# Statistics of layer 1 on the scalar engine, and a second transpose by blocks and transfers, in a one-core Newton and convolution kernel

## The chip, the core and the metric

The kernel runs on one core of a Trainium2 chip. The core has five engines with a queue each, and each queue is worked off in order: TensorE (PE, matrix products, written to PSUM), VectorE (DVE), ScalarE (ACT), GpSimd (POOL) and SyncE (SP, which here only issues DMA transfers). Sixteen DMA engines carry the transfers. The metric is the time of the device for one execution, in microseconds. The profile shows one such execution; its span is the part of it that the profiler records.

## The reference

The input x is 32 images of 32 channels of 128x128, in float32. Two layers are applied, each on a group norm with 16 groups of two channels.

```
# layer 0: x = x + sqrtm(gn(x)), five Newton-Schulz steps for each channel's 128x128 matrix
normA = sqrt(sum(A * A)); Y = A / normA; Z = I
for _ in range(5):
    T = 0.5 * (3 I - Z @ Y)
    Y = Y @ T; Z = T @ Z
sA = Y * sqrt(normA)

# layer 1: x = x + spectral_conv(gn(x)): a 2-D transform (real part), 64 x 32 modes kept,
# a product over channels with one 32x32 matrix for each mode, and the transform back
```

The group norm of layer 1 needs, for each group, the mean and the variance of what layer 0 gave.

## The kernel before

**Units.** One unit of work is four channels of one image, a tile of 128x512 (P, 4, P). There are 256 units, 8 for each image. `newton` (lines 446 to 478) runs the whole iteration of one unit as a Python generator: each `yield` ends its turn, and `yield from rest` gives up two turns. The iteration is not done step by step as in the reference: two polynomial stages, each through a quartic (`near_quartic` or `far_quartic`), and a last product give the same result.

**Rounds and lanes.** The main loop (from line 1077) goes round eight lanes. In each round every lane with a unit advances by one turn, and between lanes the other generators advance: `preps` (statistics of layer 0 for a pair of images), `norms` (normalising the inputs), `posts` (`settle` for a finished unit, then `forward`, `summed`), `specs`, `prods` and `backs` (layer 1). A new unit starts every 23/8 rounds where `is_far` holds, which is for images 1 to 18 (144 units), and every 5 rounds else (112 units). The order in which this loop emits instructions is the order on every engine (`keep_in_program_order`); no engine can overtake. What an engine has to give within a round's time decides whether PE, which is the fullest, finds its operands ready: two rounds lie between the product and the product that reads its result after one `rest`, four after two.

**A far unit, turn by turn.** `far_quartic` (421 to 442): four products of `mb` and `m` into a PSUM bank; DVE adds them to `v`; DVE transposes v by blocks of 32x32 into a tile `turn` (the `nc.vector.transpose` of line 426); four DMA transfers issued by SP (429 to 435) put the blocks into `w`, which then is, in another order of columns, the transpose of v; POOL takes mb from a multiple of the identity; after two rests PE multiplies v and w, and DVE makes `q`. In `newton`, ACT writes y (line 453) and the new m (456) from PSUM; after a rest PE transposes m with the identity (line 458: `transposed(m)`, four PE instructions) and ACT copies that out of PSUM as the new `mb`; POOL makes the new v (460); a rest; then `far_quartic` again, then the last products, and DVE adds the result to `xt` (line 475).

**After a unit.** `settle` (483 to 499) stores xt to DRAM (`mid`, from SP), lets POOL fold it for the transform, and lets DVE take two `bn_stats` of 128x256, one for each group, into `b_st`. After the eighth unit of an image `summed` (536 to 567) turns these into the group norm's scale: `moments` (199 to 215) takes means with a small product on PE, then DVE works out squares, and small products on PE sum over partitions. `forward` transforms four units at a time and `spectrum` goes on from there.

**Buffers.** PSUM is eight banks of 128x512, taken in turn by `bank()`. Tiles of a unit come from `four(tag, more)` with the number of buffers in `rooms` (309, 310): mb has 2 + 3, turn 4, xt 10 + 4 in the first part of the kernel. Tile reuse makes waits by itself. Each DMA transfer counts up one of eight semaphores, taken in turn by SP's and ACT's transfers together, and waits for the transfer eight before it. ACT issues the loads of the inputs (`fetch`, line 367, two for each unit, and `load` in `prep`, one for each unit on average).

Of the kernel before, what the change touches and what calls it, by code (L numbers as in the profile page):

```python
# [36 lines left out]
P = 128  # L37
# [17 lines left out]
EYE_V = 3.375 * SV  # L55
EYE_Q = 24.609375 * SQ
QS = 16 * SQ
FIRST = GROUPS[0] - 1
MORE = FIRST * 8 + 6
NB = 8  # L60
# [34 lines left out]
def conv_preact_kernel(  # L95
# [19 lines left out]
    nc.vector.tensor_scalar_mul(eye1[:, 0, :], ident, EYE)  # L115
    eye = eye1.to_broadcast([P, 4, P])
    eyes = []
    for n, f in (("v", EYE_V), ("q", EYE_Q)):
        e = const.tile([P, 1, P], F32, name=f"eye_{n}")
        nc.vector.tensor_scalar_mul(e[:, 0, :], ident, f)  # L120
        eyes.append(e.to_broadcast([P, 4, P]))
    eye_v, eye_q = eyes
    avg_mean = const.tile([P, P], F32, name="avg_mean")
    nc.vector.memset(avg_mean, -1.0 / 512)

    avg_v = const.tile([P, 1], F32, name="avg_v")
    nc.vector.memset(avg_v, 0.5 / (P * P))
    avg_0 = const.tile([P, 1], F32, name="avg_0")
    nc.vector.memset(avg_0, -P * P / 256)


    mid = [dram.tile([P, C, P], F32, name=f"mid{b}", tag=f"mid{b}") for b in range(B)]
# [66 lines left out]
    def moments(st, ms, tag):  # L199

        n = st.shape[1]
        f = st.rearrange("p g (e t) -> p g e t", t=3)
        nc.vector.tensor_reduce(ms, f[:, :, :, 1], AX.X, ALU.add)
        yield from pause
        pm = bank()[:, 0, 0:n]
        nc.tensor.matmul(pm, avg_mean, ms, start=True, stop=True)
        nm = small.tile([P, n], F32, tag=f"{tag}_nm", name=f"{tag}_nm", bufs=2)
        nc.vector.tensor_scalar_mul(nm, pm, 2.0)
        d = small.tile([P, n, 2], F32, tag=f"{tag}_d", name=f"{tag}_d")
        nc.vector.tensor_tensor(  # L210
            d, f[:, :, :, 1], nm[:, :, None].to_broadcast([P, n, 2]), ALU.add
        )
        nc.vector.tensor_mul(d, d, d)
        nc.vector.scalar_tensor_tensor(d, d, 128.0, f[:, :, :, 2], ALU.mult, ALU.add)
        return nm, d
# [4 lines left out]
    def kept(issued):  # L220
        return issued

    def prep(bs, made):
# [75 lines left out]
        for far in sorted({is_far(b) for b in bs}):  # L299
            of = [k for k, b in enumerate(bs) if is_far(b) == far]  # L300
            c = slice(of[0] * C, of[-1] * C + C)
            f = EYE_Q * QS if far else EYE * QF
            nc.vector.tensor_scalar_mul(nn[:, c], nn[:, c], P * (1.5 / f) ** 2)
        yield
        yield from root(nn, nc_, sn)
# [24 lines left out]
    def plus(ps, f, t, tag, more):  # L330

        s = four(tag, more)
        nc.vector.scalar_tensor_tensor(s, ps, f, t, ALU.mult, ALU.add)
        return s
# [17 lines left out]
    def transposed(t):  # L352
        ps = bank()
        for j in range(4):
            nc.tensor.transpose(ps[:, j, :], t[:, j, :], ident)
        return ps
# [61 lines left out]
        yield from rest  # L418
        return q

    def far_quartic(m, mb, v, more):

        ps = products(mb, m)
        nc.vector.scalar_tensor_tensor(v, ps, 1 / (4.5 * MS), v, ALU.mult, ALU.add)
        t = four("turn", more)
        nc.vector.transpose(blocks(t), v.rearrange("p c (i b) -> p b c i", b=4))
        w = four("w", more)
        into = w.rearrange("p c x -> p (c x)").rearrange("p (a x) -> p a x", a=4)
        for a in range(4):
            src = t[32 * a : 32 * a + 32].rearrange("p c x -> p (c x)")  # L430
            kept(
                nc.sync.dma_start(
                    out=into[:, a], in_=src.rearrange("p (b x) -> p b x", b=4)
                )
            )
        minus(eye_q, mb, mb)
        yield from rest
        yield from rest
        ps = products(v, blocks(w).rearrange("p a c j -> p c a j"))
        q = plus(ps, SQ / SV**2, mb, "q", more)  # L440
        yield from rest
        return q

# [2 lines left out]
    def newton(g, sn, xt, m, mb, v, far, more):  # L446


        qf, et, eye_t = (QS, EYE_Q, eye_q) if far else (QF, EYE, eye)
        q = yield from far_quartic(m, mb, v, more) if far else near_quartic(m, mb, more)  # L450
        my = four("my", more)
        y = my[:, :, 0, :]
        nc.scalar.mul(y, products(q, m), 1 / (MS * qf))
        yield from rest
        m = my[:, :, 1, :]
        nc.scalar.mul(m, products(q, y), MS / qf)
        yield from rest
        mb = taken(transposed(m), "mb", more)
        if far:
            v = minus(eye_v, m, four("v", more))  # L460
        yield from rest
        q = yield from far_quartic(m, mb, v, more) if far else near_quartic(m, mb, more)
        both = [bank().rearrange("p (j k) x -> p j k x", k=2) for _ in range(2)]
        for j in range(4):
            nc.tensor.matmul(both[j // 2][:, j % 2], q[:, j], my[:, j], start=True, stop=True)
        w, y = four("t", more), four("y4", more)
        for h in range(2):
            nc.scalar.mul(w[:, 2 * h : 2 * h + 2, :], both[h][:, :, 1, :], 1 / (MS * qf))
        for j in range(4):
            c = 4 * g + j  # L470
            nc.scalar.mul(y[:, j, :], both[j // 2][:, j % 2, 0, :], sn[:, c : c + 1])
        yield from rest
        t = plus(products(w, q), -0.5 * et / (1.5 * qf), eye_t, "t", more)
        yield from rest
        nc.vector.tensor_tensor(xt, products(t, y), xt, ALU.add)
        if not todo and lanes.count(None) == LANES - 1:
            warm(2)
        yield
# [4 lines left out]
    def settle(b, g, st, xt):  # L483

        kept(nc.sync.dma_start(out=mid[b][:, 4 * g : 4 * g + 4, :], in_=xt))
        if g % 2 == 0:
            folds[b, g // 2] = sets.tile([P, 8, P], F32, tag="fold", name=f"fold{b}_{g}", bufs=3)
        f = folds[b, g // 2][:, 4 * (g % 2) : 4 * (g % 2) + 4, :]
        for half, op in enumerate((ALU.add, ALU.subtract)):
            nc.gpsimd.tensor_tensor(  # L490
                f[:, :, 64 * half : 64 * half + 64], xt[:, :, 0:64], xt[:, :, 64:128], op
            )
        for j in range(2):
            at = 8 * (g // 2 % 2) + 4 * (g // 4) + 2 * (g % 2) + j
            nc.vector.bn_stats(
                st[:, at, :], xt[:, 2 * j : 2 * j + 2, :].rearrange("p c h -> p (c h)")
            )
        settled.append(rounds)
        yield
# [35 lines left out]

    def summed(b, st):

        mq = small.tile([P, 2, G], F32, tag="b_mq", name=f"b_mq{b}")
        _, d = yield from moments(st, mq[:, 0, :], "b")
        yield  # L540

        nc.vector.tensor_reduce(mq[:, 1, :], d, AX.X, ALU.add)
        wide = small.tile([P, 2, G, 2], F32, tag="b_wide", name=f"b_wide{b}")
        nc.vector.tensor_copy(wide, mq[:, :, :, None].to_broadcast([P, 2, G, 2]))
        wide = wide.rearrange("p k g c -> p k (g c)")
        yield from pause
        pv = bank()[:, 0, :]
        for i in range(4):
            rows = slice(C * i, C * i + C)
            nc.tensor.matmul(pv[rows, 0:1], wide[:, 1, :], avg_v, start=True, stop=True)  # L550
        nc.tensor.matmul(pv[0:C, 1:2], wide[:, 0, :], avg_0, start=True, stop=True)
        v = small.tile([P, 2], F32, tag="b_v", name=f"b_v{b}")
        nc.vector.tensor_scalar(v[:, 0:1], pv[:, 0:1], 1.0, EPS, ALU.mult, ALU.add)
        nc.vector.tensor_copy(v[0:C, 1:2], pv[0:C, 1:2])
        yield
        s = small.tile([P, 3], F32, tag="b_r", name=f"b_r{b}")
        nc.scalar.activation(s[:, 0:1], v[:, 0:1], AF.Sqrt)
        yield
        nc.vector.reciprocal(s[:, 1:2], s[:, 0:1])
        nc.vector.tensor_scalar(  # L560
            s[:, 2:3], v[:, 0:1], s[:, 1:2], s[:, 1:2], ALU.mult, ALU.mult
        )
        nc.vector.tensor_scalar(s[:, 2:3], s[:, 2:3], -0.5, 1.5, ALU.mult, ALU.add)
        r = small.tile([P, 1], F32, tag="b_inv", name=f"b_inv{b}")
        nc.vector.tensor_mul(r, s[:, 1:2], s[:, 2:3])
        scales[b] = v, r
        yield
# [460 lines left out]
    def end(b, g, xt):  # L1028

        if g == 0:  # L1030
            u = up.tile([P, 2, 8, 2, L], F32, tag="u", name=f"u{b}")
            st = small.tile([P, G, 6], F32, tag="b_st", name=f"b_st{b}", bufs=2)
            ended[b] = (u, st)
        u, st = ended[b]
        posts.append(settle(b, g, st, xt))
        if g == C // 4 - 1:
            posts.append(then(summed(b, st)))
        if g % 4 == 3:
            posts.append(forward(b, g // 4, u))
        if g == C // 4 - 1:  # L1040
            posts.append(last(b, u))
# [144 lines left out]
```

## Time and profile before

| | |
|---|---|
| median of 3 runs | 3018.94 us (3016.51 to 3023.95) |
| the profiled execution | 3016.65 us, of which the span is 3014.7 us |
| PE busy | 2897.6 us, 96% of the span |
| PE weight loads busy | 2689.0 us |
| DVE busy | 2321.8 us, 77% |
| POOL busy | 1995.8 us, 66% |
| ACT busy | 1652.1 us, 55% |
| DMA packets | 442482, 560.91 MB |
| chain that ended last | PE 71%, POOL 8%, DVE 7%, DMA 7%, issue 5% |

The span has two parts. Up to some 1650 us the far units run, and each stretch of 100 us has the same look: PE busy for 99 to 100 of it, DVE for 83 to 91, POOL for 71 to 75, ACT for 58 to 62, and the DMA engines for 49 to 65%. After that come the near units together with layer 1's products and inverse transforms: PE is busy for 90 to 100 of 100 us, DVE for 50 to 84, ACT for 44 to 61, and the DMA engines for up to 85%. Busy time of an engine is the union of its instructions; a busy PE is not a PE at its peak, but where one product follows the other without a gap nothing more fits in between. All lines of the kernel are put down to line 89, where a helper issues every instruction, so groups are told apart by the names of their tiles: "turn<-v" is an instruction that reads v and writes turn.

### The profile page before, as it was taken

What the parts mean: (1) busy time and instruction counts of PE and PEld (TensorE: products, weight loads), DVE (VectorE), ACT (ScalarE), POOL (GpSimd) and SP (SyncE); (2) the same over time, 40 slices, a digit from 0 to 9 for tenths busy, and PEclk for the clock granted to TensorE, in tenths of its full rate; (3) what the DMA queues carried; (4) which work ended last, traced back from release to release, by engine and by line L of the source; (5) the groups of instructions that cost most, each with busy time, mean ns of one, the idle gap of its engine ahead of it and who ended that gap; (6) DMA issues with size and microseconds to landing.
All of it is one profiled execution on the core that took longest, in us unless ns stands there. A gap on an engine that the chain in (4) does not pass through costs nothing.

```text
span 3014.7 us, 73315 instructions
## 1 busy us (share of the span) xinstructions
PE 2897.6 (96%) x27112; PEld 2689.0 (89%) x27112; DVE 2321.8 (77%) x4262; ACT 1652.1 (55%) x4187; POOL 1995.8 (66%) x2308
## 2 busy tenths in 40 slices
PE   7999999999999999999999999999989999999995
PEld 7899999999999999999999889888878899888884
DVE  7778898989888888889876645777886767776564
ACT  4566666566565656566554445455544544665452
POOL 4676777777777767777765434787777763678352
PEclk9999999999999999999999999999999999999997
DMA  5465655556565656565633566777877737676576
GB/s 176 135 176 145 171 163 153 167 152 180 134 192 135 192 131 195 142 183 140 190 102 99 158 209 208 257 247 254 271 235 245 252 121 225 203 242 216 175 230 242
DMA packets 442482, 560.91 MB, mean 186 GB/s; under 512 B 99344, under 2 KB 260112, under 8 KB 442128
## 3 DMA queue, kind: packets, MB, share of 16 engines
q1 hardware_dynamic: 328512, 347.77, 38.7%
q10 hardware_dynamic: 113616, 208.45, 22.2%
q8 instruction: 218, 3.57, 0.5%
q14 instruction: 136, 1.11, 0.1%
HBM read 326.93 MB, written 153.62 MB: 159 GB/s over the span
## 4 chain that ended last, share of the span: by engine, by line
PE 71%; POOL 8%; DVE 7%; DMA 7%; issue 5%; SPq 1%; ACT 1%; ACTq 0%; POOLq 0%; DVEq 0%
PE ps L89 71%; POOL yt L89 3%; POOL r L89 2%; POOL x L89 1%; POOL fold L89 1%; DMA yt<-mid 1%; SPq L89 1%; DVE turn L89 1%; DVE root L89 1%; DMA w<-turn 1%; DMA out<-yt 1%; DVE v L89 1%; DVE yt L89 1%; DVE a_d L89 1%; DMA xs<-in_xs 1%
## 5 line engine op out<-in xcount | busy, mean ns | idle before, releaser
L89 PE MATMUL ps<-my,q 128*128 128x128 f32 (+1 forms) x4096 | 747.0, 330 | 16.6 <-DVE q L89 9.9
L89 PEld LDWEIGHTS ps<-my,q 128*128 128x128 f32 x4096 | 623.0, 192 | 67.7 <-issue 7.4
L89 PE MATMUL ps<-w,v 128*128 128x128 f32 x4096 | 555.4, 279 | 19.6 <-DVE w L89 15.3
L89 ACT ACTIVATE b<-b,a_off,a_sc 128x128 f32<-128x128 f32 x1024 | 469.7, 491 | 166.2 <-issue 57.0
L89 ACT ACTIVATE my<-ps 128x512 f32<-128x512 f32 x512 | 306.2, 599 | 428.3 <-PE ps L89 408.9
L89 POOL TENSOR_TENSOR fold<-xt 128x256 f32<-128x256 f32 x512 | 363.4, 731 | 261.5 <-DVE xt L89 248.9
L89 PEld LDWEIGHTS ps<-w,v 128*128 128x128 f32 x4096 | 502.9, 193 | 32.5 <-DVE w L89 13.9
L89 POOL TENSOR_TENSOR yt<-yt,d 128x512 f32<-128x512 f32 x244 | 306.5, 1279 | 223.2 <-ACT d L89 195.5
L89 ACT ACTIVATE t<-ps 128x256 f32<-128x256 f32 x512 | 192.0, 381 | 311.7 <-PE ps L89 298.4
L89 DVE STREAM_TRANSPOSE turn<-v 128x512 f32<-128x512 f32 x288 | 326.1, 1132 | 9.9
L89 POOL TENSOR_SCALAR x<-xt,a_nm,a_sc 128x128 f32<-128x128 f32 x736 | 321.4, 450 | 15.6 <-DVE a_sc L89 15.4
L89 POOL TENSOR_TENSOR mb<-eye_q,mb 128x512 f32<-128x512 f32 x144 | 184.0, 1278 | 197.8 <-ACT y L89 139.2
L89 ACT ACTIVATE y<-ps,a_t_s 128x128 f32<-128x128 f32 x1024 | 290.4, 374 | 0.0
L89 POOL TENSOR_TENSOR v<-eye_v,x 128x512 f32<-128x512 f32 x144 | 184.0, 1278 | 143.8 <-ACT x L89 136.7
L89 PE MATMUL ps<-q,t 128*128 128x128 f32 x2048 | 273.9, 277 | 4.3 <-ACT t L89 3.7
L89 PE MATMUL ps<-x,b 128*128 128x128 f32 x2048 | 277.7, 279 | 0.0
L89 PE MATMUL ps<-x,q 128*128 128x128 f32 x2048 | 274.7, 277 | 3.0 <-DVE w L89 2.0
L89 DVE SCALAR_TENSOR_TENSOR v<-ps,v 128x512 f32<-128x512 f32 x288 | 195.1, 678 | 104.5 <-PE ps L89 101.8
L89 PE MATMUL ps<-y,t 128*128 128x128 f32 x2048 | 274.5, 277 | 0.1
L89 PE MATMUL ps<-my,mb 128*128 128x128 f32 x2048 | 272.2, 276 | 0.0
L89 PEld LDWEIGHTS ps<-my,mb 128*128 128x128 f32 x2048 | 257.9, 192 | 9.6 <-issue 1.6
L89 PEld LDWEIGHTS ps<-x,q 128*128 128x128 f32 x2048 | 249.4, 192 | 14.1 <-issue 8.4
(131 smaller groups left out, 5074.9 us busy)
## 6 DMA issues: line engine op xcount, KB each, us to landing
w<-turn SPq DMA_DIRECT2D x1152, 64.0 KB
b<-in_x ACTq DMA_DIRECT2D x256, 256.0 KB
xt<-in_xt ACTq DMA_DIRECT2D x256, 256.0 KB
mid<-xt SPq DMA_DIRECT2D x256, 256.0 KB
yt<-mid SPq DMA_DIRECT2D x128, 512.0 KB
xs<-in_xs ACTq DMA_DIRECT2D x252, 256.0 KB
out<-yt SPq DMA_DIRECT2D x115, 512.0 KB
plain<-in_wk SPq DMA_DIRECT2D x34, 512.0 KB
```

What stands on the lines that cost most here:

```text
L89: return self.tc.keep_in_program_order(issue(*args, **kw))
```

## The change

Two things are changed, and the first stage's iteration gets other scales for it.

- Statistics of layer 1. `settle` no longer has `bn_stats`. For each of the unit's two groups ACT runs two activations over 128x256 of xt: a Copy, whose accumulator output is the sum, and a Square with the group's (negative) mean of layer 0 as bias, whose accumulator output is the sum of squares about that mean. The elements themselves go into a tile `waste` that nothing reads. The second group's pair comes a turn later. `summed` no longer calls `moments`; it has sums of both kinds at once, copies them and the mean into `wide` (three copies on DVE), sums over partitions on PE (13 small products for each image, 5 and one of 128x16 before), and gets the variance on DVE.
- The second mb of a far unit. PE's four transposes of m and ACT's copy are gone. DVE transposes the products of q and y by blocks straight out of PSUM into a turn tile, right after ACT has been given m from the same bank, and four DMA transfers from SP put the blocks into mb, now in runs of 32 elements. The rests around it are kept. Since PSUM holds the products and not m, mb comes with another scale (`TURNED`), which the second quartic takes into account; a third identity, `eye_p`, belongs to it. Near units keep PE's transposes.

Beside this `a_nm`, the means of layer 0, has three buffers in place of two.

```diff
-    nc.vector.memset(avg_0, -P * P / 256)
+    nc.vector.memset(avg_0, -0.5)
+    avg_s = const.tile([P, 1], F32, name="avg_s")
+    nc.vector.memset(avg_s, 1 / P)
+    waste = const.tile([P, 2 * P], F32, name="waste")
...
-    def far_quartic(m, mb, v, more):
+    def across(t, into):
+        for a in range(4):
+            src = t[32 * a : 32 * a + 32].rearrange("p c x -> p (c x)")
+            kept(
+                nc.sync.dma_start(out=into(a), in_=src.rearrange("p (b x) -> p b x", b=4))
+            )
+
+    def far_quartic(m, mb, v, more, f, eye_q):
...
         w = four("w", more)
...
+        across(t, lambda a: w.rearrange("p c x -> p (c x)")[:, P * a : P * a + P])
...
         m = my[:, :, 1, :]
-        nc.scalar.mul(m, products(q, y), MS / qf)
-        yield from rest
-        mb = taken(transposed(m), "mb", more)
+        ps = products(q, y)
+        nc.scalar.mul(m, ps, MS / qf)
         if far:
+            t = four("turn", more)
+            nc.vector.transpose(blocks(t), ps.rearrange("p c (i b) -> p b c i", b=4))
+            mb = four("mb", more)
+            across(t, lambda a: mb[:, :, 32 * a : 32 * a + 32])
+            yield from rest
             v = minus(eye_v, m, four("v", more))
-        yield from rest
-        q = yield from far_quartic(m, mb, v, more) if far else near_quartic(m, mb, more)
+            yield from rest
+            qf, et, eye_t = QS * TURNED, EYE_Q * TURNED, eye_p
+            q = yield from far_quartic(m, mb, v, more, TURNED, eye_p)
+        else:
+            yield from rest
+            mb = taken(transposed(m), "mb", more)
+            yield from rest
+            et, eye_t = EYE, eye
+            q = yield from near_quartic(m, mb, more)
...
         for j in range(2):
-            at = 8 * (g // 2 % 2) + 4 * (g // 4) + 2 * (g % 2) + j
-            nc.vector.bn_stats(
-                st[:, at, :], xt[:, 2 * j : 2 * j + 2, :].rearrange("p c h -> p (c h)")
-            )
+            if j:
+                yield
+            of = xt[:, 2 * j : 2 * j + 2, :].rearrange("p c h -> p (c h)")
+            n = 2 * g + j
+            nc.scalar.activation(
+                waste, of, AF.Copy, accum_out=st[:, 0, at + j : at + j + 1]
+            )
+            nc.scalar.activation(
+                waste,
+                of,
+                AF.Square,
+                bias=made[b][0][:, n : n + 1],
+                accum_out=st[:, 1, at + j : at + j + 1],
+            )
...
-        mq = small.tile([P, 2, G], F32, tag="b_mq", name=f"b_mq{b}")
-        _, d = yield from moments(st, mq[:, 0, :], "b")
-        yield
-
-        nc.vector.tensor_reduce(mq[:, 1, :], d, AX.X, ALU.add)
-        wide = small.tile([P, 2, G, 2], F32, tag="b_wide", name=f"b_wide{b}")
-        nc.vector.tensor_copy(wide, mq[:, :, :, None].to_broadcast([P, 2, G, 2]))
+        wide = small.tile([P, 3, G, 2], F32, tag="b_wide", name=f"b_wide{b}")
+        nc.vector.tensor_copy(wide[:, 0:2], st[:, :, :, None].to_broadcast([P, 2, G, 2]))
+        for half in range(2):
+            nm = made[b][0].rearrange("p (a h c) -> p h a c", a=2, h=2)[:, half]
+            nc.vector.tensor_copy(
+                wide[:, 2, 8 * half : 8 * half + 8].rearrange("p (a c) e -> p a c e", a=2),
+                nm[:, :, :, None].to_broadcast([P, 2, 4, 2]),
+            )
...
             nc.tensor.matmul(pv[rows, 0:1], wide[:, 1, :], avg_v, start=True, stop=True)
+            nc.tensor.matmul(pv[rows, 2:3], wide[:, 0, :], avg_v, start=True, stop=False)
+            nc.tensor.matmul(pv[rows, 2:3], wide[:, 2, :], avg_s, start=False, stop=True)
```

More of the change, by code (lines that the diff above doesn't have):

```diff
@@ L57 @@
 QS = 16 * SQ
+TURNED = QS / MS
 FIRST = GROUPS[0] - 1
@@ L117, in conv_preact_kernel @@
     eyes = []
-    for n, f in (("v", EYE_V), ("q", EYE_Q)):
+    for n, f in (("v", EYE_V), ("q", EYE_Q), ("p", EYE_Q * TURNED)):
         e = const.tile([P, 1, P], F32, name=f"eye_{n}")
@@ L121, in conv_preact_kernel @@
         eyes.append(e.to_broadcast([P, 4, P]))
-    eye_v, eye_q = eyes
+    eye_v, eye_q, eye_p = eyes
     avg_mean = const.tile([P, P], F32, name="avg_mean")
@@ L206, in moments @@
         nc.tensor.matmul(pm, avg_mean, ms, start=True, stop=True)
-        nm = small.tile([P, n], F32, tag=f"{tag}_nm", name=f"{tag}_nm", bufs=2)
+        nm = small.tile([P, n], F32, tag=f"{tag}_nm", name=f"{tag}_nm", bufs=3)
         nc.vector.tensor_scalar_mul(nm, pm, 2.0)
@@ L301, in prep @@
             c = slice(of[0] * C, of[-1] * C + C)
-            f = EYE_Q * QS if far else EYE * QF
+            f = EYE_Q * QS * TURNED**2 if far else EYE * QF
             nc.vector.tensor_scalar_mul(nn[:, c], nn[:, c], P * (1.5 / f) ** 2)
@@ L419, in near_quartic @@
         return q
-    def far_quartic(m, mb, v, more):
+    def across(t, into):
[5 more added lines that the diff above has]
+    def far_quartic(m, mb, v, more, f, eye_q):
         ps = products(mb, m)
-        nc.vector.scalar_tensor_tensor(v, ps, 1 / (4.5 * MS), v, ALU.mult, ALU.add)
+        nc.vector.scalar_tensor_tensor(v, ps, 1 / (4.5 * MS * f), v, ALU.mult, ALU.add)
         t = four("turn", more)
@@ L427, in far_quartic @@
         w = four("w", more)
[L428 to L433, printed above, removed]
-                )
-            )
+        across(t, lambda a: w.rearrange("p c x -> p (c x)")[:, P * a : P * a + P])
         minus(eye_q, mb, mb)
@@ L439, in far_quartic @@
         ps = products(v, blocks(w).rearrange("p a c j -> p c a j"))
-        q = plus(ps, SQ / SV**2, mb, "q", more)
+        q = plus(ps, f * SQ / SV**2, mb, "q", more)
         yield from rest
@@ L446, in newton @@
     def newton(g, sn, xt, m, mb, v, far, more):
-        qf, et, eye_t = (QS, EYE_Q, eye_q) if far else (QF, EYE, eye)
-        q = yield from far_quartic(m, mb, v, more) if far else near_quartic(m, mb, more)
+        qf = QS if far else QF
+        if far:
+            q = yield from far_quartic(m, mb, v, more, 1.0, eye_q)
+        else:
+            q = yield from near_quartic(m, mb, more)
         my = four("my", more)
@@ L455, in newton @@
         m = my[:, :, 1, :]
-        nc.scalar.mul(m, products(q, y), MS / qf)
-        yield from rest
-        mb = taken(transposed(m), "mb", more)
+        ps = products(q, y)
+        nc.scalar.mul(m, ps, MS / qf)
         if far:
-            v = minus(eye_v, m, four("v", more))
-        yield from rest
-        q = yield from far_quartic(m, mb, v, more) if far else near_quartic(m, mb, more)
+            t = four("turn", more)
[3 more added lines that the diff above has]
+            yield from rest
+            v = minus(eye_v, m, four("v", more))
+            yield from rest
+            qf, et, eye_t = QS * TURNED, EYE_Q * TURNED, eye_p
+            q = yield from far_quartic(m, mb, v, more, TURNED, eye_p)
+        else:
+            yield from rest
+            mb = taken(transposed(m), "mb", more)
+            yield from rest
+            et, eye_t = EYE, eye
+            q = yield from near_quartic(m, mb, more)
         both = [bank().rearrange("p (j k) x -> p j k x", k=2) for _ in range(2)]
@@ L492, in settle @@
             )
+        at = 8 * (g // 2 % 2) + 4 * (g // 4) + 2 * (g % 2)
         for j in range(2):
-            at = 8 * (g // 2 % 2) + 4 * (g // 4) + 2 * (g % 2) + j
-            nc.vector.bn_stats(
-                st[:, at, :], xt[:, 2 * j : 2 * j + 2, :].rearrange("p c h -> p (c h)")
+            if j:
[11 more added lines that the diff above has]
+                accum_out=st[:, 1, at + j : at + j + 1],
             )
@@ L550, in summed @@
             nc.tensor.matmul(pv[rows, 0:1], wide[:, 1, :], avg_v, start=True, stop=True)
+            nc.tensor.matmul(pv[rows, 2:3], wide[:, 0, :], avg_v, start=True, stop=False)
+            nc.tensor.matmul(pv[rows, 2:3], wide[:, 2, :], avg_s, start=False, stop=True)
         nc.tensor.matmul(pv[0:C, 1:2], wide[:, 0, :], avg_0, start=True, stop=True)
-        v = small.tile([P, 2], F32, tag="b_v", name=f"b_v{b}")
-        nc.vector.tensor_scalar(v[:, 0:1], pv[:, 0:1], 1.0, EPS, ALU.mult, ALU.add)
+        v = small.tile([P, 4], F32, tag="b_v", name=f"b_v{b}")
+        nc.vector.tensor_copy(v[:, 2:3], pv[:, 2:3])
         nc.vector.tensor_copy(v[0:C, 1:2], pv[0:C, 1:2])
+        nc.vector.tensor_scalar(v[:, 3:4], v[:, 2:3], v[:, 2:3], -1.0, ALU.mult, ALU.mult)
+        nc.vector.tensor_scalar(v[:, 0:1], pv[:, 0:1], EPS, v[:, 3:4], ALU.add, ALU.add)
         yield
@@ L1031, in end @@
             u = up.tile([P, 2, 8, 2, L], F32, tag="u", name=f"u{b}")
-            st = small.tile([P, G, 6], F32, tag="b_st", name=f"b_st{b}", bufs=2)
+            st = small.tile([P, 2, G], F32, tag="b_st", name=f"b_st{b}", bufs=2)
             ended[b] = (u, st)
```

## The prediction

> **What bounds the kernel now.** I read the page first, then busy time by windows, the timeline of PE, what PE waited for, and the groups of instructions by shape.
>
> ```profile
> span 3014.7 us, 73315 instructions
> PE 2897.6 (96%) x27112; PEld 2689.0 (89%) x27112; DVE 2321.8 (77%) x4262; ACT 1652.1 (55%) x4187; POOL 1995.8 (66%) x2308
> ...
> 300.00:1500.00 1200.00, 1194.07 (x9977) 1133.43 (x9976) 1037.99 (x1837) 730.05 (x1870) 873.30 (x960) 1.00 0.59 163
> ```
>
> The last row is a stretch of the far units: length, then busy PE, PEld, DVE, ACT, POOL, clock, DMA share, GB/s. PE has 6 us of 1200 free, DVE 13%, ACT 39%. The chain that ended last has a period there:
>
> ```profile
> 1090.08 118.98 PE ps L89 x970
> ...
> 1250.25 118.98 PE ps L89 x972
> ```
>
> 160.2 us for two images (16 units), so 10.01 us for a unit. What PE's four transposes cost is read from starts, since matmuls overlap:
>
> ```profile
> 1004.32 1.06 PE L89 MATMUL ps<-w,v 128*128 128x128 f32 x8
> 1005.21 0.60 PE L89 MATMUL ps<-ident,my 128*128 128x128 f32 x4
> 1005.64 1.06 PE L89 MATMUL ps<-my,q 128*128 128x128 f32 x8
> ```
>
> From 1005.21 to 1005.64: 0.43 to 0.44 us, under half of four products. What PE waited for in 300 to 1500, then DVE in the worst stretch of a period:
>
> ```profile
> PE ps L89 <- DVE a_d L89: 2.9, 7, 0.4
> PE ps L89 <- DVE q L89: 2.3, 7, 0.3
> PE ps L89 <- ACT my L89: 0.8, 1, 0.8
> ...
> 1200.00:1256.00 56.00, 55.28 (x468) 52.45 (x467) 53.36 (x93) 35.48 (x93) 39.64 (x45) 1.00 0.49 131
> ```
>
> PE hardly waits, but DVE is the one it waits for: the seven waits on a_d and on q come once a period, where `prep`'s small operations pile onto DVE. In these 56 us DVE waits 1.5 us in all. From the end of DVE's q to the next product that reads it there are often 3 us, but in this stretch 0.1 to 2; behind ACT's m, t and mb there are usually 4 to 5 (starts and ends of the trace). So PE sets the pace, DVE is a hair behind, ACT has room. The rows for the change:
>
> ```profile
> L89 DVE STREAM_TRANSPOSE turn<-v 128x512 f32<-128x512 f32 x288 | 326.1, 1132 | 9.9
> L89 DVE BATCH_NORM_STATS2 b_st<-xt 128x6 f32<-128x256 f32 x512 | 189.6, 413 | 0.3
> L89 ACT COPY mb<-ps 128x512 f32<-128x512 f32 x256 | 149.7, 585 | 177.8 <-PE ps L89 161.7 <-DMA w<-turn 6.1 <-POOL yt L89 2.5
> L89 DVE STREAM_TRANSPOSE u<-ps 128x512 f32<-128x512 f32 x64 | 45.5, 710 | 12.9 <-PE ps L89 12.8
> ...
> L89 SPq DMA_DIRECT2D w<-turn x1152: 542/602/1984, 90.8 to 1556.4; - x192
> ```
>
> [...] ACT's d and DVE's yt read one bank, and ACT waited 20.8 us, 37 times, for DVE yt. So DVE's new transpose waits for ACT's m. [...] The trace has 381 for t<-ps with 256 elements[...]. [...] The packet records here show 34.7 ns for 512 bytes, 18.5 for 256 and 13.1 for 128.
>
> **The change, part by part.** Sums are against the profiled execution (3016.65 us with 3014.7 in the span; the median is 2.3 us higher).
>
> PE: 144 far units lose 0.436 us, −62.8 us; a far period becomes 160.2 − 16 x 0.436 = 153.2 us. The eight more tiny products of an image follow each other at some 10 ns an instruction, so +0.2 us an image: 5 us in all at most, mostly in PE's gaps; I take nothing.
>
> DVE, for a period: 138.8 us busy. Away: 32 `bn_stats` (11.9 us at 0.37 busy), and for each image moments and squares (some 1.9 us, less 1.1 for the copies and the variance that come): −13.5. New: 16 block transposes from PSUM. No row has a strided read of PSUM. Low end 0.71 us (u<-ps, no stride penalty)[...]; I take 1.2[...]: +19.2[...]. DVE then has 144.5 us of 153.2, 94%. The average fits, the bad stretch doesn't: PE would now need 56 − 56/10.01 x 0.436 = 53.6 us for it, DVE's 53.4 lose 10 `bn_stats` and an image's moments (−4.5) and gain 5.6 transposes and the new copies (+7.5): 56.4, and 0.1 us was left ahead of PE. The 2.8 us of excess come out as waiting of PE, and up to 1.5 more if DVE's own waits stay (2.8 to 4.3). I take 3.5 x 9 periods = +31.5 us (at 0.71 for a transpose: 0.7 us, +6[...]).
>
> ACT, for a unit: 6.1 us; mb away in far units, −0.585. New: two Copies[...] and two Squares with a bias pointer[...], each waiting for the one before it because of `waste`[...], plus whatever the accumulator's read-out costs. No row shows that; I take 0.1 to 0.25 us for each of four (bounds 0 and 0.5): 2.2 to 2.8. ACT goes to 7.7 to 8.3 of 9.57 us, plus some 0.3 where it issues DMAs: 84 to 90%. It stays under PE, but its queue now blocks in two new places: the first Copy waits for DVE's xt (at that place in ACT's order ACT came before xt was ready in 30 of 120 far units, by up to 2.7 us), and y, m and t stand behind. Their slack of 4 to 5 us hides most. I take +5 us in far units. In the near part nothing leaves PE; 112 units put 0.25 of ACT's time more in, where t has 3.2 us to spare at the median, 1.6 at its worst twentieth, and DVE loses 0.74 us a unit. I take +10 us (from −10, where DVE's w and t held PE, to +30).
>
> SP and DMA: twelve rather than eight transfers for a unit; at 0.62 us an issue SP goes from some 5.5 to 7.9 us of 9.57. Their 512-byte runs become 128 bytes: 2048 packets x 13.1 ns / 16 = 1.7 us of all engines a unit (2.4 at the 256-byte price), so the share goes from 0.59 to about 0.80. mb has four rounds (13.3 us); DVE's lag of 2 to 5, its transpose, four issues (2.5) and the landing (2.3, up to 6.8) make 8 to 13: hidden, barely at its worst. As a transfer waits for the eighth before it, ACT's loads stand behind w's sooner: 5 to 6 us of PE's time after it rather than 8 to 9. I count that in ACT's 5 us. `turn` has four buffers for three uses a unit (two before), 12.8 us of reuse against some 7 of life.
>
> Sum: −62.8 + 31.5 + 5 + 10 = −16.3, 3000.4 us; at the level of the median 3002.
>
> **Rivals.** *The full gain.* [...] DVE then has less work than before and PE keeps 153.2 us: −63 + 6 + 5 = −52, 2967. For it: u<-ps at 710. Against: turn<-v at 1132. *A wash.* DVE waits for ACT's m whenever it is up to date, and its 9 free microseconds a period go to that (16 x 0.5): the period stays near 160, 3010 to 3028. *Slower: ACT paces.* The four statistics with their read-outs, and the waits of an in-order queue for xt and for earlier transfers, reach 4.2 us a unit; 5.5 + 0.3 + 4.2 = 10.0 is today's pace, so from there on far units are slower than before, and the near part pays in full. At 4.6 us: +0.4 x 144, +20 near, −10 for what waits coincide: 3085; about 3050 at 4.3. For it: ACT waits on DVE and DVE on ACT in turn. [...] *Transfers late.* The DMA share stands at 0.92 in the worst 10 us of a period; with 0.2 more it is full for some 60 us of each, mb and the loads land late: 4 us past the gain in each period, 3035.
>
> **How the numbers follow.** DVE takes half (2985 to 3010): 0.36. Full gain (2950 to 2985): 0.10. Wash: 0.14. ACT paces (3028 to 3080): 0.30. Transfers late (3028 to 3050): 0.10. Runs of this kernel spread by 0.25%, so 0.3% (9 us) tells from no change: faster 0.46, same 0.14, slower 0.40. The range leaves out half of the full gain and the upper part of ACT's case: 2965 to 3055. The likeliest case's own range is 2985 to 3010.
>
> **What would show it.** Right: far periods of 156 to 158 us; DVE over 92% there, turn<-ps near 1.2 us; new waits of PE on DVE q and a_d of 3 to 4 us a period, nothing on mb's transfers; ACT at 80 to 85%. Wrong: waits of PE on ACT my or t; DVE's turn waiting for ACT my by more than 10 us a period; a second period above 160; mb<-turn issues well above 0.62 us on SP.

## The result and the profile after

The changed kernel takes 3107.8 us (3103.5 to 3111.1), against 3018.4 (3016.5 to 3024.0) for the kernel before: a ratio of 1.029, 95% interval 1.027 to 1.031. It is 89 us slower. 3002 was forecast.

In the two profiled executions all of it lies in the far units. The last transfer into w is issued at 1644.2 us instead of 1556.4, 87.8 us later; what follows it takes 1457.5 us instead of 1458.3. The page of the changed kernel, its stretch from 300 to 1500 us (length, then busy PE, PEld, DVE, ACT, POOL, granted clock, DMA share, GB/s), and what PE waited for there (total, times, longest):

```profile
span 3101.7 us, 75862 instructions
PE 2877.4 (93%) x26984; PEld 2649.5 (85%) x26984; DVE 2214.0 (71%) x3832; ACT 2050.5 (66%) x6091; POOL 1996.9 (64%) x2308
...
PE 54%; DMA 14%; POOL 9%; DVE 6%; issue 6%; ACT 6%; SPq 4%; ACTq 1%; DVEq 0%; POOLq 0%
...
300.00:1500.00 1200.00, 1106.56 (x9118) 1039.77 (x9118) 955.77 (x1587) 836.12 (x2551) 820.52 (x903) 0.98 0.72 177
```

```profile
PE ps L90 <- ACT my L90: 43.5, 12, 6.2
PE ps L90 <- DMA mb<-turn: 13.9, 9, 2.9
PE ps L90 <- DVE q L90: 13.6, 10, 2.0
PE ps L90 <- DVE xt L90: 6.8, 8, 1.0
PE ps L90 <- DMA w<-turn: 5.9, 8, 1.3
```

No engine is full in this stretch: PE 92%, DVE 80%, ACT 70%, POOL 68%, the DMA engines 72%. PE had 6 us free before and has 93 now. In the chain that ended last PE fell from 71% to 54% and DMA rose from 7% to 14%. So nothing replaced PE as the bound. What PE waits for comes late, most of all ACT's m. The rows of what the change added, grouped by shape, with busy time and mean ns of one, then the idle time before it; of SP the issues, shortest, median and longest:

```profile
L90 DVE STREAM_TRANSPOSE turn<-ps 128x512 f32<-128x512 f32 x144 | 102.4, 711 | 165.6 <-ACT my L90 145.3 <-DMA w<-turn 20.0
L90 ACT ACTIVATE waste<-xt 128x256 f32<-128x256 f32 x512 | 216.7, 423 | 83.8 <-DVE v L90 18.1 <-DMA mb<-turn 9.9 <-DMA b<-in_x 9.3
L90 ACT ACTIVATE waste<-xt,a_nm 128x256 f32<-128x256 f32 x512 | 260.4, 509 | 16.6
L90 ACT ACTIVATION_READ_ACCUMULATOR waste<-xt 128x1 f32 x512 | 104.1, 203 | 0.0
L90 ACT ACTIVATION_READ_ACCUMULATOR waste<-xt,a_nm 128x1 f32 x512 | 95.5, 186 | 0.0
...
L90 SPq DMA_DIRECT2D w<-turn x1152: 542/602/2265, 94.0 to 1644.2; - x192
L90 SPq DMA_DIRECT2D mb<-turn x576: 609/632/3177, 114.2 to 1632.4; - x192
```

The own prices of the additions are small: 0.711 us for the block transpose out of PSUM, and for a pair of statistics 0.423 + 0.203 + 0.509 + 0.186, of which neighbours overlap somewhat.

**One stall, followed back.** One of PE's long waits for ACT's m shows how it comes about. The timelines of PE, ACT and SP in the changed kernel (start, length, engine, what, and in brackets the idle time before it with its releaser):

```profile
1045.91 1.09 PE L90 MATMUL ps<-fold,tab 128*32 128x504 f32 x12
1051.52 2.08 PE L90 MATMUL ps<-my,q 128*128 128x128 f32 x8 [4.52 <-ACT my L90]
...
1041.92 5.96 ACTq L90 DMA_DIRECT2D xs<-in_xs  x3
1047.92 0.49 ACT L90 ACTIVATE b<-b,a_off,a_sc 128x128 f32<-128x128 f32 x1 [5.84 <-DMA mid<-xt]
...
1049.09 0.40 ACT L90 ACTIVATE waste<-xt 128x256 f32<-128x256 f32 x1
...
1050.89 0.57 ACT L90 ACTIVATE my<-ps 128x512 f32<-128x512 f32 x1
...
1040.19 4.80 SPq L90 DMA_DIRECT2D mb<-turn  x4
1045.04 0.63 SPq L90 DMA_DIRECT2D mid<-xt  x1
```

PE waits 4.5 us for ACT's m. ACT stood 5.8 us at a load of xs, issued at 1047.54. By the instruction records the 3469 transfers of SP and ACT count on eight semaphores, and this load on the same one as SP's store of xt into mid before it, of which the chain has the landing at 1047.52. SP issued that store only at 1045.04, behind four transfers of mb that held SP for 4.8 us (the chain has their first released by POOL's x, at 1041.98). After that ACT works off what had piled up: three normalisations, a pair of statistics, two more, and then m, 3 us after it was free. SP's lateness has passed into ACT through a semaphore, with no data between them.

This is no single case. Between 300 and 1500 us PE waits seven times for ACT's m for 4.5 to 6.2 us, once in every period of 16 units; these make 36.6 of its 43.5 us. Each of the seven ends 3.6 us after a stop of ACT, of 5.5 to 7.1 us, for the landing of a store into mid (total, times, longest):

```profile
ACT b L90 <- DMA mid<-xt: 47.5, 10, 7.1
```

The stall then costs more than itself. The same stretch in windows of 2 us, with PE first (busy, matmuls) and the granted clock third from the end:

```profile
1046.00:1048.00 2.00, 1.00 (x12) 0.31 (x12) 2.00 (x5) 0.08 (x1) 0.00 (x0) 1.00 0.82 228
1048.00:1050.00 2.00, 0.00 (x0) 0.00 (x0) 1.17 (x4) 1.97 (x6) 0.00 (x0) 1.00 0.86 248
1050.00:1052.00 2.00, 0.48 (x2) 0.48 (x3) 0.94 (x2) 1.47 (x5) 1.25 (x2) 0.71 0.73 194
1052.00:1054.00 2.00, 2.00 (x11) 2.00 (x11) 0.00 (x0) 0.37 (x1) 1.25 (x2) 0.50 0.46 143
1054.00:1056.00 2.00, 2.00 (x12) 2.00 (x11) 1.74 (x4) 1.27 (x5) 0.61 (x1) 0.50 0.45 140
1056.00:1058.00 2.00, 2.00 (x12) 2.00 (x12) 1.31 (x2) 0.68 (x2) 2.00 (x3) 0.58 0.55 76
1058.00:1060.00 2.00, 2.00 (x13) 1.79 (x12) 1.65 (x2) 0.80 (x2) 1.63 (x3) 1.00 0.95 245
```

From 1050.8 to 1057.6 us PE has half its clock: 11 or 12 matmuls in 2 us, where the windows of 2 us from 1060 to 1066 us, at full clock, have 21 each. From its first matmul at 1051.5 on that is some 3 us lost on top of 4.5. Between 300 and 1500 us the clock is at half nine times, four times for 3.41 us and five times for 6.83, which makes 47.8 us. Seven of the nine follow the waits for ACT's m, but two follow waits of only 2.2 and 2.9 us. All nine begin on one grid of 3.41 us. In the step of the grid just before, PE was busy for nothing at the seven, and for 58 and 27% at the two, so the clock fell there without a whole step of idle time. The kernel before has none in that stretch.

The sum for that stretch: 93.4 us idle against 5.9, and 0.02 of 1200 = 24 us of clock (some 3 of them while PE stood anyway), so at most 112 lost more; 0.436 us for each of some 114 units saved, 50 (9118 PE instructions at 80.2 a unit; before 9977 for 119.9 units, so 83.2, less four and plus one). Net at most 62 in 1200 us, or 0.54 for a unit and 78 for 144, against 85 measured from the first to the last transfer into w.

### The profile page after: what moved, and what is told of

Read it like the earlier page. It is cut to its first block, busy times and chain, and to the rows that moved or that the text cites. A ratio compares the mean times of both kernels' runs of the same rounds, so it can differ in the third digit from the quotient of the medians.

```text
span 3101.7 us, 75862 instructions
## 1 busy us (share of the span) xinstructions
PE 2877.4 (93%) x26984; PEld 2649.5 (85%) x26984; DVE 2214.0 (71%) x3832; ACT 2050.5 (66%) x6091; POOL 1996.9 (64%) x2308
## 4 chain that ended last, share of the span: by engine, by line
PE 54%; DMA 14%; POOL 9%; DVE 6%; issue 6%; ACT 6%; SPq 4%; ACTq 1%; DVEq 0%; POOLq 0%
PE ps L90 54%; DMA w<-turn 5%; SPq L90 4%; POOL yt L90 3%; DMA mb<-turn 2%; POOL fold L90 2%; DMA yt<-mid 2%; POOL r L90 2%; POOL x L90 2%; DMA mid<-xt 2%; ACT b L90 1%; ACT waste L90 1%; ACT y L90 1%; ACTq L90 1%; ACT x L90 1%
## 5 line engine op out<-in xcount | busy, mean ns | idle before, releaser
L90 PE MATMUL ps<-my,q 128*128 128x128 f32 (+1 forms) x4096 | 758.8, 334 | 78.7 <-ACT my L90 58.4
L90 PEld LDWEIGHTS ps<-my,q 128*128 128x128 f32 x4096 | 629.9, 195 | 132.8 <-ACT my L90 63.3
L90 PE MATMUL ps<-w,v 128*128 128x128 f32 x4096 | 545.9, 278 | 47.5 <-DMA mb<-turn 15.9
L90 DVE STREAM_TRANSPOSE turn<-v 128x512 f32<-128x512 f32 x288 | 324.2, 1126 | 9.8
L90 ACT ACTIVATE t<-ps 128x256 f32<-128x256 f32 x512 | 182.5, 378 | 198.8 <-PE ps L90 191.6
L90 PE MATMUL ps<-my,mb 128*128 128x128 f32 x2048 | 280.3, 281 | 12.5 <-ACT mb L90 5.8
L90 PEld LDWEIGHTS ps<-my,mb 128*128 128x128 f32 x2048 | 264.3, 196 | 25.1 <-ACT mb L90 6.4
L90 DVE SCALAR_TENSOR_TENSOR w<-ps,r 128x512 f32<-128x512 f32 x224 | 153.3, 684 | 176.5 <-POOL r L90 96.7
L90 ACT ACTIVATE waste<-xt 128x256 f32<-128x256 f32 x512 | 216.7, 423 | 83.8 <-DVE v L90 18.1
L90 ACT ACTIVATE waste<-xt,a_nm 128x256 f32<-128x256 f32 x512 | 260.4, 509 | 16.6
```

The costliest lines, as they stand in the source:

```text
L90: return self.tc.keep_in_program_order(issue(*args, **kw))
```

## The experiments

My first theory was that the queues take slack from each other, so that each part of the change alone would cost little. The rivals were ACT's statistics, the transfers of mb, and DVE's waiting for ACT (110.7 us of 1200). Each expectation below is as it stood before its run. All results, with the last issue of a transfer into w as the end of the far part, and from 300 to 1500 us the waiting of ACT for transfers, of PE in all, of PE for transfers and of SP in all (sums over the waits in each trace; trace columns come from one execution each, whose far end can stand some 10 us from that of another):

| run | us | ratio to before (95%) | far end | ACT, transfers | PE, all | PE, transfers | SP, all |
|---|---|---|---|---|---|---|---|
| before | 3018 | 1 | 1556 | 41 | 6 | 0 | 522 |
| the change | 3108 | 1.027-1.031 | 1644 | 133 | 93 | 20 | 228 |
| stats_only | 3064 | 1.013-1.016 | 1595 | 52 | 33 | 0 | 544 |
| mb_only | 3055 | 1.009-1.013 | 1597 | 176 | 61 | 11 | 208 |
| dve_first | 3151 | 1.041-1.050 | 1685 | 143 | 109 | 4 | 258 |
| dummy | 3096 | 1.023-1.027 | 1633 | 156 | 42 | 0 | 208 |
| dummy_tiny | 3053 | 1.009-1.013 | 1594 | 107 | 26 | 0 | 221 |
| dummy_two | 3071 | 1.016-1.021 | 1605 | 83 | 30 | 0 | 341 |
| mb_sp | 3196 | 1.057-1.061 | 1751 | 0 | 140 | 21 | 116 |
| act_filler | 3054 | 1.011-1.014 | 1591 | 58 | 36 | 0 | 549 |
| mb_pool | 3044 | 1.007-1.013 | 1595 | 112 | 64 | 33 | 199 |
| after_pool | 3063 | 1.013-1.020 | 1600 | 34 | 66 | 37 | 172 |
| mb_rest | 3140 | 1.039-1.043 | 1661 | 158 | 102 | 26 | 235 |
| before_rest | 3054 | 1.011-1.014 | 1574 | 38 | 18 | 0 | 509 |
| before_pool3 | 3029 | 1.002-1.006 | 1561 | 0 | 10 | 2 | 531 |
| stats_pool3 | 3020 | 1.000-1.001 | 1574 | 0 | 12 | 0 | 521 |
| mb_pool3 | 3053 | 1.009-1.015 | 1581 | 0 | 53 | 28 | 151 |
| after_pool3 | 3052 | 1.009-1.014 | 1592 | 0 | 62 | 32 | 147 |
| half_pool3 | 3038 | 1.005-1.008 | 1581 | 0 | 41 | 22 | 352 |
| quarter_pool3 | 3017 | 0.998-1.001 | 1552 | 0 | 14 | 1 | 416 |

**Each part alone.** stats_only puts the diff's `settle` and `summed` into the kernel before; mb_only is the changed kernel with the old ones.

> The kernel before with the first part of the change alone: layer 1's statistics on ACT, mb still by PE's four transposes and ACT's copy. Measured from the kernel before (3018). Theory (the queues block each other and each part takes slack from the other): +10 to +30 us, well under the 89 of the whole change. Rival, ACT's 2.65 us of statistics for a unit are the cause by themselves: +60 to +100. Rival, the transfers of mb are the cause: within 10 us of the kernel before.

> The changed kernel with bn_stats on DVE again, so the second part of the change alone: the second mb by DVE's block transposes and four transfers. Measured from the kernel before (3018). Theory of queues that block each other: -20 to +30 us. Rival, ACT's statistics are the cause: -62.8 of PE's time or most of it shows, -60 to -40. Rival, the transfers (eight under way at most, SP's issues, the share of the DMA engines): +50 to +90.

Measured +44 and +36, together 80 of the 89. Both lie above the range of my first theory and below those of the rivals. That theory falls, since the parts nearly add up. And both cost. For mb that means that PE's gain of 63 us is lost and 36 more, so that its transfers cost some 99.

**DVE ahead of ACT.**

```diff
-        nc.scalar.mul(m, ps, MS / qf)
         if far:
             t = four("turn", more)
             nc.vector.transpose(blocks(t), ps.rearrange("p c (i b) -> p b c i", b=4))
+        nc.scalar.mul(m, ps, MS / qf)
...
```

> The changed kernel with one thing exchanged: DVE's block transpose out of PSUM stands before ACT's m in program order, so that DVE no longer waits for ACT (111 us of waiting on ACT's my between 300 and 1500 us) and ACT waits 0.71 us for DVE instead. Rival, DVE's wait for the bank that ACT holds is the cause: 40 to 90 us less than the changed kernel's 3108. Theory of queues in general: 0 to 25 us less, since ACT's m, of which PE waits, comes later by DVE's part. If it is slower than 3108, ACT's queue is the tighter one.

43 us slower than the changed kernel: DVE's waiting for ACT was the largest new wait on DVE, but taking most of it away gains nothing, since ACT now waits for DVE (its m for turn: 104.1 us from 300 to 1500). PE's waiting for ACT went from 52 to 97 us: ACT's m is the tighter of the two.

**Transfers that nothing needs**, in the kernel before, right after ACT's m.

```diff
...
+        if far:
+            for a in range(4):
+                src = q[32 * a : 32 * a + 32].rearrange("p c x -> p (c x)")
+                kept(nc.sync.dma_start(
+                    out=dump[:, :, 32 * a : 32 * a + 32],
+                    in_=src.rearrange("p (b x) -> p b x", b=4)))
```

> The kernel before with four more transfers in each far unit, at the place where the changed kernel has those of mb, of the same shape (runs of 32 elements), from q into a tile that nothing reads. They wait for nothing that is late and nothing waits for their data; they only take SP's time, one of the eight places each, and the DMA engines. Measured from the kernel before (3018). Rival, the transfers' load and places are the cause: +40 to +90. Theory that it is lateness of results (ACT's m, DVE's turn, mb) and not the load: 0 to +20.

Measured +77. That is the transfers' price by itself, without DVE's transpose and with no product that needs their data. The trace of this run has ACT waiting for transfers 156 us instead of 41 and DVE 85 instead of 15. ACT's largest are for the dummies and for w (12 us before):

```profile
ACT b L89 <- DMA dump<-q: 45.2, 16, 5.7
ACT b L89 <- DMA w<-turn: 41.9, 37, 2.4
ACT b L89 <- DMA b<-in_x: 24.0, 8, 5.4
```

Two variants take the load or half of the number away: `out=dump[rows, 0, 0:32], in_=q[rows, 0, 0:32]` four times, and two transfers of every other run of 32 elements.

> The kernel before with four more transfers in each far unit at the same place as in the run with mb-like transfers that nothing reads (which cost 77 us), but each of them only 32 rows of 128 bytes: 128 packets for a unit instead of 2048, so next to no load on the DMA engines, but four of SP's issues and four of the eight places as before. Measured from the kernel before (3019). Theory that the places (each transfer waits for the eighth before it, ACT's loads too) or SP's issues are what costs: +40 to +80. Rival, the load of 128-byte packets on the DMA engines is what costs: 0 to +15.

> As the run with mb-like transfers that nothing reads, with the same 2048 packets of 128 bytes for a unit, but in two transfers instead of four, row to the same row. Measured from the kernel before (3019). Theory of the places and of SP's issues: about half of the 77 us or less, +15 to +45. Rival, the load of the packets: +60 to +90.

+34 and +52, both between the ranges of the two theories, so neither holds alone. Four nearly empty transfers cost 34, some 8.5 each. If number and load simply add, the load of the packets costs 77 − 34 = 43 by the one run and 52 − 17 = 35 by the other. How the 34 are split between SP's issues (a median of 0.59 us for the empty ones too) and the places was not told apart.

**ACT's loads and ACT's work.** mb_sp issues the loads of `fetch` and `prep` from SP; act_filler leaves the kernel before as it is and adds the four activations on a constant.

> The second part of the change alone (statistics on DVE; 3055 with ACT's loads on ACT), with the loads of the inputs issued by SP instead of ACT: three issues less on ACT for a unit, and ACT is never blocked by an earlier transfer; SP has 15 to 16 issues a unit, 8.5 to 9 us of 10. Theory that ACT, blocked at its loads by the eight places, makes PE's operands late: 2985 to 3030. Rival, SP as a queue is the tight one (its issues and what it waits for): 3080 or more. Near part of either: within 20 us of before.

> The kernel before with the same four activations for a unit at the same place on ACT (2.65 us), but on a constant, so that they wait for nothing but each other; the statistics stay on DVE too. Measured from the kernel before (3019); the real statistics on ACT alone gave +44. Theory that ACT's time itself, put ahead of y, m and t in one queue, makes them late: +35 to +60. Rival, the wait for DVE's xt in ACT's queue is what costs: 0 to +20.

mb_sp: +141 over mb_only. ACT waits for no transfer any more and PE hardly for ACT (1.7 us), but SP's queue is the tight one now: xs comes late, DVE's `bn_stats` waits 150 us for it, and q behind it. act_filler: +35 of the 44, so the wait for DVE's xt is not the main part. I read this as ACT's own work being the cost; the last group of runs shows that this reading was wrong.

**Loads from POOL.** Between 300 and 1500 us ACT waits 50.5 us for landings of xs in mb_only; in mb_pool, where POOL issues xs, neither ACT nor SP waits for one. One line moves xs:

```diff
-            kept(nc.scalar.dma_start(out=t, in_=src))
+            kept((nc.gpsimd if first_b else nc.scalar).dma_start(out=t, in_=src))
```

> The second part of the change alone (statistics on DVE; 3055), with the loads of xs, one for a unit, issued by POOL instead of ACT. POOL's transfers have semaphores of their own, so xs takes none of the eight places and ACT is blocked at two loads for a unit instead of three; SP's queue is left as it was. POOL gets one issue a unit more. Theory that the eight places, through ACT's queue, make a good part of the loss: 3020 to 3042. Rival, SP's queue and the load of the packets make it, or POOL's queue is delayed as much: 3050 or more.

> The whole change (3108), with the loads of xs issued by POOL instead of ACT. Theory of the eight places through ACT's queue: 15 to 45 us less than 3108, more than what the same edit gives where the statistics are on DVE, since ACT is fuller here. Rival, ACT is late by its own work and not by waits for transfers: within 10 us of 3108.

−11 for mb alone (3044, between the two ranges), −45 for the whole change, half of its loss.

**More time for mb.** One `yield` more ahead of the second `far_quartic`, and FAR = 24/8.

> The second part of the change alone (3055), with one turn more between the transfers of mb and the product that reads it, and units started every 24/8 rounds instead of 23/8, so that eight lanes still hold one unit each: mb has five rounds instead of four. Theory that mb itself comes late (four rounds are too few): 3010 to 3040. Rival, the losses are at all the waits of the queues and not at mb: 3050 to 3080, since each round is now 4% shorter and every other distance with it.

> The kernel before with the same extra turn and 24/8 rounds between starts, as a control. If rounds 4% shorter cost nothing where the queues have slack: 3010 to 3030. If they cost: 3030 to 3060, and that much of what the other kernel with the extra turn shows is due to the shorter rounds and not to mb.

mb_rest is 85 us slower than mb_only, outside both ranges; a fifth round for mb was no help. The control says part of why: the same work with rounds 4% shorter and one turn more costs 36 us, 18 of it in the far part. The other 49 of the 85 stay open. My reading of the control: distances are fixed in rounds, and a round is as long as PE's work makes it. Taking 4% of PE's work away shortens them all alike, so a gain on PE is in part paid for with the cover of everything else. The added turn also holds a unit's tiles for longer, and that was not tested apart.

**All loads of far units from POOL.**

```diff
-        kept(nc.scalar.dma_start(out=t, in_=x[b, :, 4 * g : 4 * g + 4, :]))
-        kept(nc.scalar.dma_start(out=xt, in_=xt_in[b, :, 4 * g : 4 * g + 4, :]))
+        queue = nc.gpsimd if is_far(b) else nc.scalar
+        kept(queue.dma_start(out=t, in_=x[b, :, 4 * g : 4 * g + 4, :]))
+        kept(queue.dma_start(out=xt, in_=xt_in[b, :, 4 * g : 4 * g + 4, :]))
```

> The whole change, with all three loads of a far unit (b, xt, xs) issued by POOL, whose transfers have semaphores of their own: ACT issues no transfer in the far part, and SP's transfers wait only for SP's. Theory that ACT stuck at a load, whose place an SP transfer issued late still holds, is what makes PE stall: less than the 3063 that xs alone on POOL gave, 3005 to 3050. Rival, POOL (0.56 us an issue, waits for tiles in its order) is late instead, or ACT is late by its own work: 3060 or more.

> The second part of the change alone (statistics on DVE; 3055, and 3044 with xs on POOL), with all three loads of a far unit on POOL. Theory of ACT stuck at its loads: 3010 to 3040. Rival, SP's queue, the load of the packets and DVE's work make the remaining loss: 3040 to 3060.

> The kernel before with all three loads of a far unit on POOL, as a control. Both theories: within 12 us of 3018, since PE waits for nothing there; slower by more than that would say that POOL's issues cost by themselves.

> The first part of the change alone (statistics on ACT; 3063), with all three loads of a far unit on POOL. Theory that ACT's own work, put ahead of y, m and t, costs (a constant's activations cost 35 of the 44): 3040 to 3065. Rival, ACT's loads and their waits turn that work into a loss: 3015 to 3035.

The control costs 10 us. Against it the statistics on ACT come out 9 lower where they had cost 44, so at 3020 they are level with the kernel before. In the profiled executions, each slower than its median, the far part still ends 13 us after the control's (39 later than before with the loads on ACT), and what follows is 17 shorter; so what is shown is that most of the cost is gone, not a gain in the far part. The stretch of stats_pool3 and what PE waited for in it, then a line of stats_only:

```profile
300.00:1500.00 1200.00, 1187.76 (x10094) 1126.40 (x10093) 953.86 (x1545) 932.08 (x2802) 1053.14 (x1308) 1.00 0.57 161
...
PE ps L89 <- DVE q L89: 9.3, 8, 1.4
PE ps L89 <- DVE u L89: 1.8, 1, 1.8
PE ps L89 <- ACT my L89: 0.7, 1, 0.7
...
PE ps L89 <- ACT my L89: 8.5, 7, 1.8
```

ACT is at 78% and PE waits for it once, 0.7 us, where stats_only had 23 us of waits for ACT. So ACT's work costs little where ACT issues no loads. Moving the loads also takes their issues off ACT, some 0.33 us each (xs in the changed kernel: median 0.335). That alone is too little: the filler paid 35 us for some 2.1 us of work a unit, at which price one load less would be worth 6 us (an estimate), and moving xs gave 45. How work and loads add up is my reading: the work fills the time in which ACT used to make up for a stop at a load. The filler on a constant had both as well, which is why it could not tell them apart. The whole change comes to 3052, as mb alone does. mb alone gains almost nothing from the move, 3055 to 3053, against 3010 to 3040 if ACT's stops had been its cost; of 89 us the move takes away 56, and the 33 that remain come with mb. What is left is another thing: in after_pool3 ACT waits for no transfer, and PE waits for these:

```profile
PE ps L90 <- DMA w<-turn: 18.3, 12, 4.0
PE ps L90 <- DMA mb<-turn: 13.9, 10, 3.3
PE ps L90 <- DVE q L90: 11.1, 8, 1.7
```

SP has 147 of 1200 us left there in which it waits for anything.

**Fewer units by transfers.** `if g % 2:` (or `g % 4 == 3`) around the transpose and the transfers, else `mb = taken(transposed(m), "mb", more, TURNED)`.

> The whole change with all loads of a far unit on POOL (3052), but only every other far unit's second mb goes by DVE's block transposes and transfers; the others have PE's four transposes and ACT's copy again (in the other scale). SP has two issues a unit less on average, PE 31 us of transposes back. If the cost of mb's transfers is in proportion to their number: 3036, half way between 3020 (statistics alone, loads on POOL) and 3052. Theory that SP's queue, nearly full, makes w and mb late, so that the cost grows faster than the number: 3000 to 3028. Rival, any late result costs, full queue or not: 3036 or more.

> As the run with half of the units, but only each fourth far unit has its second mb by transfers (36 of 144); PE's transposes cost 47 of the 63 us. In proportion: 3028. Theory of SP's full queue: 3000 to 3018, since SP has slack for one issue more a unit, and PE's 16 us come out as a gain.

3038 and 3017, after 3020 with none and 3052 with all. The half is near where proportion puts it (3036), the quarter is below (3028) and in the range of the theory of SP's full queue, which the half is not. PE's waiting for transfers is 1, 22 and 32 us, SP's free time 416, 352 and 147, so PE's waits rise early and not only when SP is full. A full queue of SP is not the whole cause; how much is due to SP's order, the load of the 128-byte packets or irregular arrival stays open. quarter_pool3 is the fastest of the variants, and not to be told from the kernel before. No variant beat that kernel.

## Why the prediction was wrong

- *PE, −62.8.* About right. Units at full clock take (1106.6 − 20.5) / 113.7 = 9.55 us of PE instead of 9.96.
- *DVE, +31.5.* Wrong in its mechanism. The 1.2 us for a transpose was my estimate; it took 0.711 us, the low end, as the rival of the full gain needed it, and DVE is 80% busy and not 94%. That the stride of four elements costs as much out of PSUM as out of SBUF was not shown: with that stride turn<-v takes 1126 ns from SBUF and turn<-ps 711 from PSUM, where u<-ps without it takes 707. PE's waits for DVE did grow, from 5 to 20 us in 1200, so some of the 31.5 came true, but not because DVE was full.
- *ACT's own work.* About right: 2.2 to 2.8 us were forecast, my estimate. The four means and read-outs add up to 2.64, but they overlap: by starts a pair takes 1.03 (1049.09 to 1050.12), so a unit 2.1, where each was taken to wait for the one before it. ACT is at 70%, not 84 to 90, as the pace is slower.
- *"As a transfer waits for the eighth before it, ... I count that in ACT's 5 us."* This step failed. Its coupling was seen and priced at next to nothing; with the loads on ACT the statistics cost 44 us, with the loads on POOL they come out level with the kernel before. The slack of 4 to 5 us behind m, t and mb was taken as free for ACT's work, while stops of up to 7.1 us at the loads used the same slack.
- *SP and DMA: "hidden, barely at its worst".* Also failed. The sizes were about right (an issue 0.632 for 0.62; the DMA engines 0.72 x 10.55 − 0.59 x 10.01 = 1.7 us more a unit, as forecast; SP without a wait for (1200 − 228) / 114 = 8.5 us a unit, where 7.9 was forecast), but what was asked was only whether mb arrives in time. In the kernel before, transfers whose data nobody needs cost 77 us, with ACT and DVE waiting longer for the other transfers. And with the loads on POOL the products do wait for mb and w, 32 us in 1200. Which part of SP's queue and the packets makes them late stays open.
- *Near part, +10.* Wrong: −0.8.
- *The rivals.* "ACT paces" had the waits "for earlier transfers" in it, but asked for 4.2 us a unit of statistics and waits until ACT sets the pace; ACT's busy time grew by some 1.8 us a unit (836.1/114 − 730.1/120 + 0.585 for the copy of mb that is gone) and its waits for transfers by 0.8, so it did not set the pace, it held PE up at single places. "Transfers late" reached to 3050 at most. Both took place, one through the other, and my range let only one happen. Of the signs named for a wrong forecast three came: PE waited for ACT's my, DVE for ACT's my 15.6 us a period (110.7 x 169/1200), and a period came to 10.6 x 16 = 169 us. The fourth did not: mb's issues stayed at a median of 0.632 us. Of the signs for a right one none came in the size named.
- *Missing altogether:* the clock after a long stall, some 20 us in 1200, and, as I read the control, the rounds that shrink with PE's work.

## What to carry over

Where an engine both computes and issues transfers, ask what each issue waits for, and whose queue that stands in: a free share of 40% is no slack if the engine may stand for 7 us at a place that another queue holds. Price added transfers by what they do to the others, for instance with transfers that nothing reads, before asking whether their own data comes in time. Where distances are fixed in rounds, expect a shorter round to take cover from every step at once, and run a control for it.

## What was not expected of the hardware

A block transpose of 128x512 out of PSUM with a stride of four elements took 711 ns, while from SBUF the same one takes 1126 to 1132. Reading out ACT's accumulator is an instruction of its own, 186 to 203 ns. In the changed kernel a wait of PE of 4.5 us was followed by 6.83 us at half the granted clock, and waits of 2.2 and 2.9 us by 3.41 and 6.83. A load issued by POOL takes 0.54 to 0.56 us of POOL, against 0.33 for one on ACT, and with xs issued by POOL (mb_pool) neither ACT nor SP waited for it from 300 to 1500 us, where ACT had waited 50.5 us (mb_only).
